# MLP first layers: the lo halves made by GpSimd from SBUF, their factor folded in at the start, and another share for the work beside attention

## Chip, core and metric

The kernel runs on one core of one Trainium2 chip. The metric is the time of the program on the device in microseconds (us). The engines are named as in the profile: PE is TensorE, DVE is VectorE, ACT is ScalarE, POOL is GpSimd, SP is SyncE, which issues the DMAs here.

## What is computed

The input x is 4 x 1024 x 256 in float32. Three residual steps follow each other: half a mixture-of-experts layer, a transformer block, and half the mixture-of-experts layer again.

```python
x = x + 0.5 * ffn(layernorm(x))
x = x + attn(layernorm(x))
x = x + 0.5 * ffn(layernorm(x))

# attn, per batch: 16 heads of 64, 1024 rows
q, k, v = (ln(x, s, b) @ W + bias for each of the three)
p = softmax(q @ k.T / 16 + mask)          # mask: one corner element, -999
h = (p @ v) @ Wo + bo + x
y = ln(h, lnm_s, lnm_b)
m = gelu(y @ W1 + b1) @ W2 + b2           # tanh form of gelu; W1 is 256 x 512
return m + h

# ffn: 8 experts with the best 2 weighted, and a shared one, 256 -> 128 -> 256, exact gelu
```

The change is in the line `m = gelu(y @ W1 + b1) @ W2 + b2`, the MLP of the transformer block.

## The kernel before

**Precision.** Matmul operands are split into two float16 numbers, hi and lo, where hi is the rounded value and lo the rest. A product is three matmuls: hi by hi, hi by lo, lo by hi (`mm3`, L974 to L978, whose matmuls all carry the line L970). Every operand made on the chip therefore costs two operations: one that writes hi and one that subtracts hi from the full value.

**Tiling.** A batch has 8 pairs of heads; for each pair q, k and v are projected, and then come 4 units (a head and a half of its queries) of 4 steps. In all there are 4 x 8 x 4 x 4 = 512 attention steps. A step i has these parts:

- `maxima` (L1444): scores of 128 queries into PSUM slot 0 (L1464), whose row maximum DVE takes (L1471). After four of them `row` (L1495) turns the maxima into a row (L1498, L1502) that a DMA puts into the tile `low`.
- `scores` (L1509): the transposed scores, already less the maximum, into PSUM slot 1 (L1528, L1529). ACT takes the exponential into `pt` (L1534, run in the helper at L570) and rounds it to `pk` hi (L1540). POOL makes `pk` lo, 128 x 1024 (L1543).
- `values` (L1564): 24 small matmuls of `pk` with V (L1578, L1580, L1581). The first two of each three need `pk` hi, the third needs `pk` lo. DVE normalises after four steps (L1593, L1594).

**Work beside attention.** Everything else is written as generators that ask for an engine and a duration (`yield Ask("DVE", 0.69)`) and are run by a planner, the class `Order` (L102). The planner fixes the order of the instructions on each engine when the program is built; it keeps a plan time per engine and takes the asks in the order of their readiness. Ahead of and behind the scores of each step, `order.share(SHARE)` (L1727, L1734) gives TensorE's plan a budget of SHARE us of other work: projections of the next pair, output projections (L1748), the expert layers of the next and the previous batch, and the MLP. Where attention isn't ready, other work is taken too. On POOL an ask of such a chain may go ahead of a waiting L1543 when that is made later by no more than LPOOL = 2.3 us of plan time (SLOW = 0.7 for rank 2).

**The resources.** PSUM has two slots of 1024 columns for scores, one place for values, and three banks of 512 columns, tag F, for all other work (`F_`, L332; `free`, L335, tells the planner that one is free). The SBUF tag `u` has BU = 3 buffers of 512 float32 columns, which MLP chunks and experts share.

**The MLP.** A job is half a batch, 512 rows. `prep` (L1837) makes the layernorm and the transposed input; it also loads x1d into `ld` buffers and lets POOL add it and the bias b2 to h (L1851, L1853). `burst` (L1856) runs the first layer in 4 chunks c of 128 hidden columns, each one bank of 512 rows, and starts a chain `gelu_tanh` (L1809) for each. `second` (L1880) runs the second layer in 4 tiles of 128 rows, each of which needs hi and lo of all 4 chunks. A chunk's chain before:

- L1814, ACT: the bank u becomes the layer's output, scaled, plus the bias `mb1`
- L1816, ACT: v (SBUF) = the square of u; L1818, DVE: v = (v + 1/c) u
- L1820, ACT: tanh of v (run at L570)
- L1822, DVE: u = (v + 1) u, in the bank
- L1824, ACT: hi = 8 u; L1826, DVE: lo = 8 u - hi; only then is the bank free (L1827)

There are 8 MLP jobs, 32 chunks. Those of the first three batches run beside attention; both of the last batch run behind the last value matmul, together with three halves of expert layers. The expert layers' own first layers (`layer`, L1128) already have their lo part made by POOL from SBUF (L1183) where they run beside attention.

**mb1.** `bias_cols` (L626) makes the bias of the first layer during the setup: a matmul, a DMA to memory and back, and a multiplication by a factor (L648), which is 1.0 here (L868).

Of the kernel before, what the change touches and what calls it, by code (L numbers as in the profile page):

```python
# [10 lines left out]
AF = mybir.ActivationFunctionType  # L11
ALU = mybir.AluOpType
# [12 lines left out]
MH = 512  # L25
EPS = 1e-5

CX = 4.0
# [6 lines left out]
CW1 = 32.0  # L35
CG = 16.0
# [14 lines left out]
KW = 8  # L51
RANK, RREST = -2, -3
WAIT, AGE, LATE, LPOOL, SLOW = 2.0, 0.2, 1.6, 2.3, 0.7
SHARE, RATE, LEAD, NEAR, OWED = 0.7, 0.58, 40, 20, -16.0
BLD = 2
BU = 3
BGB = 3
# [8 lines left out]
GELU_C = 0.044715  # L66
# [241 lines left out]
class Kernel:  # L308
# [342 lines left out]
    def setup(self):  # L651

        nc, a, cp, ap, order = self.nc, self.a, self.cp, self.ap, self.order
# [159 lines left out]
        def all_qkv():  # L813
            self.stored = [0] * 3
            order.start(qkv(0), -7)
            order.start(qkv(1), -7)
            order.start(qkv(2), -7)
            yield Ask("IF", lambda: sum(self.stored) == 6)
            order.start(others(), 5)
            yield Ask("IF", lambda: all(f"bias{n}" in self.biases for n in "qkv"))  # L820
            yield Ask("DMA", 3.0)
            self.bqkv = [self.biases[f"bias{n}"] for n in "qkv"]
            self.qkv_set = order.seen

        def kept(parts, dram, at):
            t = self.tile(ap, [P, 2, S], F16, "pk", bufs=BPK)

            def to():
                for l in range(2):
                    dma(dram[l, :, at:at + S], t[:, l])  # L830

            yield from self.split(parts, t[:, 0], t[:, 1], to)
            self.setup_left -= 1

        def others():

            self.wod = self.tile(self.dp, [2, P, 8 * D], F16, "wod")
            self.mwd = self.tile(self.dp, [2, P, 2 * 2 * MH], F16, "mwd")
            wo = [self.tile(ap, [P, S], F32, "pt", bufs=BPT)[:] for i in range(2)]
            for i in range(2):  # L840
                dma(wo[i].rearrange("p (c n) -> p c n", c=4), a["Wo"][i * 4 * P:(i + 1) * 4 * P, :].rearrange("(c p) n -> p c n", p=P))
            self.bo = self.row_bcast(a["bo"], D, "bo")
            s, bc = self.cols(a["lnm_s"], 2, "lnms"), self.cols(a["lnm_b"], 2, "lnmb")
            w1, w2 = self.tile(ap, [P, S], F32, "pt", bufs=BPT)[:], self.tile(ap, [P, S], F32, "at", bufs=BAT1)[:]
            dma(w1.rearrange("p (c n) -> p c n", c=2), a["W1"].rearrange("(c p) n -> p c n", p=P))
            dma(w2.rearrange("p (c n) -> p c n", c=4), a["W2"].rearrange("(c p) n -> p c n", p=P))
            self.mb2 = self.row_bcast(a["b2"], D, "mb2")
            yield Ask("DMA", 6.0)
            jobs = [([(wo[i], None, CWO)], self.wod, i * S) for i in range(2)]
            jobs.append(([(w1[:, k * MH:(k + 1) * MH], s[:, k:k + 1], CW1) for k in range(2)], self.mwd, 0))  # L850
            jobs.append(([(w2, None, CW2)], self.mwd, S))
            for job in jobs:
                order.start(kept(*job), 5)
            yield Ask("IF", lambda: self.qkv_set)
            bv = self.tile(ap, [P, NPAIR, P], F32, "aT", bufs=BAT)
            yield Ask("DVE", 1.1)
            nc.vector.tensor_copy(bv[:], self.bqkv[2][:].unsqueeze(2).to_broadcast([P, NPAIR, P]))
            yield Ask("BANK")
            ps = self.F_()[:, :D]
            for c in range(NPAIR):  # L860
                if c % 2 == 0:
                    yield Ask("PE", 0.9)
                nc.tensor.matmul(ps, bv[:, c, :], wo[c // 4][:, c % 4 * D:c % 4 * D + D], start=(c == 0), stop=(c == NPAIR - 1))
            yield Ask("DVE", 0.42)
            nc.vector.scalar_tensor_tensor(self.bo[:], ps, 1.0 / AV, self.bo[:], ALU.mult, ALU.add)
            self.free()
            self.bo_ready = order.seen
            order.start(self.bias_cols([w1[:, :MH], w1[:, MH:]], bc, 1.0, a["b1"], "mb1"), 5)  # L868
            yield Ask("IF", lambda: "mb1" in self.biases)
            self.mb1 = self.biases["mb1"]  # L870
            self.setup_left -= 1
# [937 lines left out]
    def gelu_tanh(self, u, c, hp, job):  # L1809

        nc = self.nc
        v = self.tile(self.mp, [P, 512], F32, "u", bufs=BU)[:]
        yield Ask("ACT", 0.67)
        nc.scalar.activation(u, u, AF.Identity, bias=self.mb1[:, c:c + 1], scale=1.0 / (CX * CW1))  # L1814
        yield Ask("ACT", 0.6)
        nc.scalar.activation(v, u, AF.Square)  # L1816
        yield Ask("DVE", 0.69)
        nc.vector.scalar_tensor_tensor(v, v, 1.0 / GELU_C, u, ALU.add, ALU.mult)  # L1818
        yield Ask("EXP", 0.63)
        self.tabled(v, v, AF.Tanh, scale=GELU_C * math.sqrt(2.0 / math.pi))  # L1820
        yield Ask("DVE", 0.69)
        nc.vector.scalar_tensor_tensor(u, v, 1.0, u, ALU.add, ALU.mult)  # L1822
        yield Ask("ACT", 0.6)
        nc.scalar.mul(hp[:, 0], u, CG / 2)  # L1824
        yield Ask("DVE", 0.69)
        nc.vector.scalar_tensor_tensor(hp[:, 1], u, CG / 2, hp[:, 0], ALU.mult, ALU.subtract)  # L1826
        self.free()  # L1827
        self.u_live -= 1
        job.left -= 1

# [97 lines left out]
```

## Time and profile before

| | us |
|---|---|
| median of 3 runs (2074.29 to 2075.26) | 2075.26 |
| profiled execution, its own time | 2072.14 |
| its span, first to last instruction | 2070.3 |
| TensorE busy in the span | 1968.2 |
| VectorE, ScalarE, GpSimd busy | 1411.7, 1500.8, 1498.1 |
| span up to the first `pk` lo (setup, first experts, first pair) | 161 |
| attention steps, to the last value matmul | 161 to 1918 |
| behind it: the last MLP and expert halves | 1918 to 2070.3 |
| mean granted TensorE clock, share of full | 0.989 |

The share of an engine is an average over stretches with different work. POOL, for example, is busy through the attention steps and almost idle behind 1918 us. Lines of groups read: line, engine, operation, output <- input, partitions x elements, count | busy us, mean ns of one | idle time of the engine just ahead of them, and what ended it. Lines of waits read: who waited, for whom: us in total, times, the longest.

### The profile page before, as it was taken

The page shows a single profiled execution, that of the slowest core. Times are in us where ns is not written, and L with a number is a line of the kernel's source. Part 1 is how long each engine was busy: PE and PEld are TensorE (multiplying, and loading weights), DVE is VectorE, ACT ScalarE, POOL GpSimd, SP SyncE. Part 2 cuts the span into 40 slices and gives each one's busy share as a digit, 9 for nine tenths or more (in the row PEclk, how much of TensorE's full clock was granted, in tenths as well). Part 3 has the DMA queues.
Part 4 walks back from the last instruction along what each step waited for, and adds up shares of the span by engine and source line. Part 5 has one row for each costly group of instructions (what it writes and reads, how often), then busy time and mean ns, then how long its engine had stood idle before and what let it go on. Part 6 is the DMA issues. An engine that isn't in the chain of part 4 may idle for free.

```text
span 2070.3 us, 53013 instructions
## 1 busy us (share of the span) xinstructions
PE 1968.2 (95%) x22468; PEld 1286.2 (62%) x22468; DVE 1411.7 (68%) x2372; ACT 1500.8 (72%) x1785; POOL 1498.1 (72%) x979
## 2 busy tenths in 40 slices
PE   6989999999999999999999999999999999999689
PEld 2546576766666566666666666656675666667356
DVE  6576676766767677776767568677677577764654
ACT  6437878778766787788787778687868787777553
POOL 7737787768767988778687987878776888778300
PEclk9999999999999999999999999999999999999899
DMA  6543233333613315243333333323233324241000
GB/s 174 151 128 84 75 91 95 76 85 68 143 35 80 86 32 113 48 113 73 85 81 81 95 75 80 96 70 75 70 69 92 103 46 107 50 103 27 21 1 31
DMA packets 213019, 166.21 MB, mean 80 GB/s; under 512 B 140991, under 2 KB 172872, under 8 KB 212782
## 3 DMA queue, kind: packets, MB, share of 16 engines
q1 hardware_dynamic: 212782, 162.83, 32.1%
q8 instruction: 176, 2.88, 0.6%
q14 instruction: 61, 0.50, 0.1%
HBM read 70.18 MB, written 13.83 MB: 41 GB/s over the span
## 4 chain that ended last, share of the span: by engine, by line
PE 79%; POOL 6%; ACT 5%; DVE 4%; DMA 3%; issue 2%; SPq 1%; POOLq 0%; DVEq 0%; ACTq 0%
PE F L970 31%; PE S L1528 10%; PE S L1464 10%; PE S L1529 9%; PE av L1581 6%; PE av L1580 5%; PE av L1578 5%; POOL pk L1543 3%; PE S L970 2%; ACT pt L570 1%; DMA gb<-gd 1%; ACT pk L1540 1%; POOL hp L1183 1%; PE S L1498 1%; POOL h L1851 1%
## 5 line engine op out<-in xcount | busy, mean ns | idle before, releaser
L1543 POOL TENSOR_TENSOR pk<-pt,pk 128x1024 f16<-128x1024 f32 x512 | 1087.8, 2133 | 258.7 <-ACT pk L1540 167.8
L1471 DVE TENSOR_REDUCE mx<-S 128x1 f32<-128x1024 f32 x512 | 626.1, 1223 | 305.4 <-PE S L1464 280.5
L570 ACT ACTIVATE pt<-S 128x1024 f32<-128x1024 f32 x512 | 523.8, 1023 | 355.4 <-PE S L1529 336.8
L1540 ACT CAST pk<-pt 128x1024 f16<-128x1024 f32 x512 | 534.7, 1045 | 15.8 <-DMA aT<-pk 0.6
L1581 PE MATMUL av<-V,pk 128*128 128x65 f16 x4096 | 428.8, 192 | 25.2 <-POOL pk L1543 24.1
L1580 PE MATMUL av<-V,pk 128*128 128x64 f16 x4096 | 435.1, 195 | 0.0
L1578 PE MATMUL av<-V,pk 128*128 128x65 f16 x4096 | 434.1, 193 | 0.7 <-DVE at L1594 0.7
L1578 PEld LDWEIGHTS <-pk 128*128 128x128 f16 x4096 | 382.1, 96 | 53.9 <-issue 0.3
L1580 PEld LDWEIGHTS <-pk 128*128 128x128 f16 x4096 | 380.4, 97 | 52.9 <-issue 1.1
L1581 PEld LDWEIGHTS <-pk 128*128 128x128 f16 x4096 | 379.9, 99 | 30.3 <-POOL pk L1543 30.0
L1528 PE MATMUL S<-low 128*128 128x512 f16 x1024 | 388.2, 379 | 6.2 <-ACT pt L570 5.5
L1529 PE MATMUL S<-AC 128*128 128x512 f16 x1024 | 388.4, 379 | 0.0
L1464 PE MATMUL S<-AC 128*128 128x512 f16 x1024 | 304.2, 378 | 8.2 <-DVE mrow L1502 4.8
L970 PEld LDWEIGHTS <-hp 128*128 128x128 f16 x2100 | 205.6, 98 | 78.2 <-issue 10.5
L970 PE MATMUL F<-xA,wq 128*128 128x512 f16 x768 | 187.6, 381 | 0.1
L970 PE MATMUL F<-wfs,hp 128*128 128x256 f16 x1404 | 178.0, 275 | 5.9 <-ACT u L570 3.7
L1529 PEld LDWEIGHTS <-AC 128*128 128x128 f16 x1024 | 99.9, 98 | 115.3 <-issue 27.6
L1528 PEld LDWEIGHTS <-low 128*128 128x128 f16 x1024 | 99.9, 98 | 104.0 <-issue 0.4
L1183 POOL TENSOR_TENSOR hp<-u,hp 128x512 f16<-128x512 f32 x88 | 100.7, 1159 | 78.5 <-ACT hp L1180 71.9
L970 PEld LDWEIGHTS <-wfs 128*128 128x128 f16 x864 | 84.3, 99 | 109.7 <-issue 20.7
L970 PE MATMUL F<-xF,wfs 128*128 128x512 f16 x522 | 127.1, 388 | 5.7 <-DVE gb L642 4.2
L970 PEld LDWEIGHTS <-wq 128*128 128x128 f16 x768 | 74.9, 98 | 84.6 <-issue 2.6
(239 smaller groups left out, 2544.8 us busy)
## 6 DMA issues: line engine op xcount, KB each, us to landing
AC<-qk SPq DMA_DIRECT2D x128, 256.0 KB
gb<-gd SPq DMA_DIRECT2D x88, 256.0 KB
low<-qk SPq DMA_DIRECT2D x64, 256.0 KB
wq<-wqd SPq DMA_DIRECT2D x33, 384.0 KB
hp<-mwd SPq DMA_DIRECT2D x6, 1024.0 KB
x<-in_L_attn_x_dram SPq DMA_DIRECT2D x8, 512.0 KB
x1d<-x SPq DMA_DIRECT2D x8, 512.0 KB
wo<-wod SPq DMA_DIRECT2D x16, 256.0 KB
```

The lines of the kernel that those rows point to most:

```text
L570: i = self.nc.scalar.activation(out, in_, func, **kw).ins
L970: i = self.nc.tensor.matmul(*args, start=start, **kw).ins
L1183: nc.gpsimd.tensor_tensor(hp[e][:, 1], u, hp[e][:, 0], ALU.subtract)
L1464: mm(ps[:, hs], AC[:, 0, qs], AC[:, 1, hs], start=True, stop=(h == 0 or t > 0), skip_group_check=True)
L1471: nc.vector.tensor_reduce(self.mx[:, t % 4:t % 4 + 1], ps, AX.X, ALU.max, negate=True)
L1528: mm(o, low[:, 1, ks], low[:, 0, qs], start=True, stop=False, skip_group_check=True)
L1529: mm(o, AC[:, 1, ks], AC[:, 0, qs], start=False, stop=True, skip_group_check=True)
L1540: nc.scalar.copy(pk[:, 0], pt[:])
L1543: nc.gpsimd.tensor_tensor(pk[:, 1], pt[:], pk[:, 0], ALU.subtract)
L1578: mm(o[:, 0:65], pk[:, 0, ps], v[:, 0:65], start=(n == 0 and c == 0 and t == 0), stop=False, skip_group_check=True)
L1580: mm(o[:, 0:64], pk[:, 0, ps], v[:, 65:129], start=False, stop=False, skip_group_check=True)
L1581: mm(o[:, 0:65], pk[:, 1, ps], v[:, 0:65], start=False, stop=(n == 3 and c == 1), skip_group_check=True)
```

## The change

The chunk's chain carries the factor 8 from its beginning, DVE's second operation writes v in SBUF and not the bank, the bank is freed there, hi is a plain copy of v, and POOL subtracts hi from v to make lo. `mb1` gets the same factor. SHARE goes from 0.70 to 0.68.

```diff
-SHARE, RATE, LEAD, NEAR, OWED = 0.7, 0.58, 40, 20, -16.0
+SHARE, RATE, LEAD, NEAR, OWED = 0.68, 0.58, 40, 20, -16.0
...
-            order.start(self.bias_cols([w1[:, :MH], w1[:, MH:]], bc, 1.0, a["b1"], "mb1"), 5)
+            order.start(self.bias_cols([w1[:, :MH], w1[:, MH:]], bc, CG / 2, a["b1"], "mb1"), 5)
...
         yield Ask("ACT", 0.67)
-        nc.scalar.activation(u, u, AF.Identity, bias=self.mb1[:, c:c + 1], scale=1.0 / (CX * CW1))
+        nc.scalar.activation(u, u, AF.Identity, bias=self.mb1[:, c:c + 1], scale=CG / 2 / (CX * CW1))
         yield Ask("ACT", 0.6)
-        nc.scalar.activation(v, u, AF.Square)
+        nc.scalar.activation(v, u, AF.Square, scale=2 / CG)
...
-        self.tabled(v, v, AF.Tanh, scale=GELU_C * math.sqrt(2.0 / math.pi))
+        self.tabled(v, v, AF.Tanh, scale=2 / CG * GELU_C * math.sqrt(2.0 / math.pi))
         yield Ask("DVE", 0.69)
-        nc.vector.scalar_tensor_tensor(u, v, 1.0, u, ALU.add, ALU.mult)
+        nc.vector.scalar_tensor_tensor(v, v, 1.0, u, ALU.add, ALU.mult)
+        self.free()
         yield Ask("ACT", 0.6)
-        nc.scalar.mul(hp[:, 0], u, CG / 2)
-        yield Ask("DVE", 0.69)
-        nc.vector.scalar_tensor_tensor(hp[:, 1], u, CG / 2, hp[:, 0], ALU.mult, ALU.subtract)
-        self.free()
+        nc.scalar.copy(hp[:, 0], v)
+        yield Ask("POOL", 1.16)
+        nc.gpsimd.tensor_tensor(hp[:, 1], v, hp[:, 0], ALU.subtract)
         self.u_live -= 1
         job.left -= 1
```

CG is 16. The lines after the change: the copy is L1825 and POOL's subtraction L1827. The buffer v is in use until that subtraction has read it; the counter `u_live` counts it to the end of the chain, before and after.

## The prediction

> **What bounds the kernel now.** I read the page first: busy shares, slices, the chain that ended last.
>
> ```profile
> span 2070.3 us, 53013 instructions
> PE 1968.2 (95%) x22468; PEld 1286.2 (62%) x22468; DVE 1411.7 (68%) x2372; ACT 1500.8 (72%) x1785; POOL 1498.1 (72%) x979
> PE   6989999999999999999999999999999999999689
> POOL 7737787768767988778687987878776888778300
> PE 79%; POOL 6%; ACT 5%; DVE 4%; DMA 3%; issue 2%; SPq 1%; POOLq 0%; DVEq 0%; ACTq 0%
> ```
>
> TensorE is busy 95% of the span and makes 79% of the chain; it is full but for the first and the last slices. The change leaves its 22468 matmuls as they are, so only its idle time, 2070.3 - 1968.2 = 102 us, can move. The table by stretches places it: 30.1 us between 715 and 1918 us (1203.0 less 1172.9 busy), and 28.3 us behind 1918 us, after the last value matmul (152.3 less 124.0). Before 715 us nothing changes (see below). Next, the waits of TensorE:
>
> ```profile
> PE av L1581 <- POOL pk L1543: 24.1, 24, 1.7
> PE S L1528 <- ACT pt L570: 5.5, 13, 1.1
> PE S L1464 <- DVE mrow L1502: 4.8, 7, 0.9
> PE F L970 <- DVE hp L1826: 2.0, 2, 1.8
> PE F L970 <- DVE pt L1826: 0.7, 1, 0.7
> ```
>
> The columns are us in total, times, longest. The largest named wait is that of the value matmuls (L1581) for the lo parts that POOL makes (L1543): 24 times. So POOL, 72% busy, is the engine whose lateness TensorE feels most, and the change gives it more work. The waits that the change can take away, for a PSUM bank held until L1826, are two, 1.75 and 0.70 us of the last two lines (the third, 0.2 us, is for the lo part itself), both behind 1918 us.
>
> The groups give the prices (busy and mean ns, then idle before and its releaser):
>
> ```profile
> L1543 POOL TENSOR_TENSOR pk<-pt,pk 128x1024 f16<-128x1024 f32 x512 | 1087.8, 2133 | 258.7 <-ACT pk L1540 167.8 <-issue 29.5 <-PE S L1529 22.9
> L1183 POOL TENSOR_TENSOR hp<-u,hp 128x512 f16<-128x512 f32 x88 | 100.7, 1159 | 78.5 <-ACT hp L1180 71.9 <-PE S L1529 4.8
> L1180 ACT CAST hp<-u 128x512 f16<-128x512 f32 x88 | 52.4, 613 | 14.1 <-DVE u L1168 14.1
> L1822 DVE SCALAR_TENSOR_TENSOR F<-u,F 128x512 f32<-128x512 f32 x32 | 22.0, 688 | 8.8 <-ACT u L570 8.3
> L1826 DVE SCALAR_TENSOR_TENSOR hp<-F,hp 128x512 f16<-128x512 f32 x28 | 19.0, 683 | 3.8 <-ACT hp L1824 3.6
> L1824 ACT ACTIVATE hp<-F 128x512 f16<-128x512 f32 x28 | 16.4, 591 | 0.3 <-DVE F L1822 0.3
> ```
>
> Last, the six stretches in which MLP first layers run beside attention; the columns are stretch, its length, then busy us (and instructions) of PE, PEld, DVE, ACT and POOL, the granted clock, DMA share, GB/s:
>
> ```profile
> 731.10:762.20 31.10, 29.04 (x337) 17.24 (x336) 23.64 (x33) 26.24 (x35) 26.10 (x19) 1.00 0.18 43
> 1351.30:1401.20 49.90, 46.98 (x584) 29.96 (x583) 37.43 (x52) 45.93 (x60) 38.31 (x19) 1.00 0.30 73
> 1646.70:1685.00 38.30, 36.77 (x440) 22.35 (x439) 28.89 (x41) 32.46 (x40) 36.17 (x28) 1.00 0.23 53
> sum 243.40, PE 232.89 PEld 145.63 DVE 183.34 ACT 211.13 POOL 191.56; mean PE 38.81 PEld 24.27 DVE 30.56 ACT 35.19 POOL 31.93
> ```
>
> Here TensorE is idle 10.5 us of 243, and 8.3 of these are waits for L1543. ACT is the fullest helper (211 of 243), POOL next (192).
>
> **The change part by part.** There are 32 chunks of 512 columns (8 MLP halves of 4): 24 in the six stretches, 8 behind 1918 us.
>
> (1) DVE loses the 32 lo operations (28 in the row above, 4 more into other tiles): 32 x 0.683 = 21.9 us, 24 x 0.683 = 16.4 in the six stretches. DVE is not the bound there (183 of 243). Idle of TensorE there that is not L1543's is 10.5 - 8.3 = 2.2 us; the gain lies between 0 and 2.2. I take 0.7, since only the waits for a row maximum are DVE's.
>
> (2) The hi part becomes a copy from SBUF instead of a scaled read of PSUM: 613 ns (L1180) for 591, 24 x 0.022 = 0.5 us on ACT, which stands ahead of L1540. Between 0 and 0.5; 0.3 taken. L1822 writes SBUF: its neighbour L1818, which does so, takes 0.680 for 0.688. The new scale operands (L1816, the tanh) and mb1's factor stand in instructions that ran before: 0, as no instruction is added; mb1's own is one of 0.135 us at 154.8 us.
>
> (3) The bank is free after L1822, not after L1826. In the 24 chunks that is 4.2 us earlier of 13.1 us (means from the start of L1814). TensorE waited for no such bank before 1918 us, so the gain there is 0; if one becomes the limit, it is at most those 2.2 us.
>
> (4) POOL gains 32 x 1.159 = 37.1 us (L1183 is the same operation), 24 x 1.159 = 27.8 in the six stretches: 191.6 + 27.8 = 219.4 of 243.4, still below the stretch. But two stretches run over: 26.1 + 4.6 = 30.7 of 31.1, and 36.2 + 4.6 = 40.8 of 38.3, where the 16 operations L1304 and L1309 of the next batch's h fall too. The queue behind an added operation is L1543, and behind that the value matmuls; the buffer v is also held until POOL is done. To price it, I took the order in which the instructions of both programs stand. For each attention step I summed the TensorE work between the end of its scores and its first value matmul (its cover, at 0.217 us per 512 columns, as in runs of 12 matmuls in 2.59 us), and the other POOL work queued just ahead of its L1543. Then I read from the trace what each kind of step waits for L1543, over steps 8 to 511:
> cover under 5.3 us with other POOL work ahead: 18 steps, 13.88 us, 0.771 each; after: 23 steps.
> cover under 5.3 us, none ahead: 57 steps, 0.056 each; after: 54.
> longer cover, over 1.7 us ahead: 41 steps, 0.133 each; after: 42.
> the rest: 388 steps, 0.009 each; after: 385.
> So 25.9 us become 17.7 + 3.0 + 5.6 + 3.3 = 29.6, +3.7. With the cover cut finer (at 4.3, 5.3 and 6.1 us) it is 27.3, +1.5. I take +2.0, nearer the finer cut. Bounds: -4 (half of the 8.3 gone, as the order is another one) and +11 (24 x 0.46, the rate of the finer class with a cover of 4.3 to 5.3 us and over 1.7 us of other POOL work ahead).
>
> The Trainium skill speaks against this part: "GPSIMD Engine Reference", Engine selection, puts elementwise work of two inputs on VectorE, GpSimd being about 2x slower. The rows here say 1159 for 683 ns, 1.7x. By the rule, each move costs the difference, and 24 of them in line would be 11 us slower; by the rows above, POOL has room in four of six stretches and the sum is +2.
>
> (5) The share 0.68. The order of the changed program is that of before until the 169th score step, near 740 us, on TensorE and likewise on the others: no effect before it. Behind it, with the lo parts moved and the share left at 0.70, the same count gives 35 to 38 us of waits; with the share at 0.68 alone, 25 to 27. So the share takes back most of what POOL's load costs, and (4) holds it already. The work left behind the last value matmul is 818 matmuls in both, so nothing is pushed to the end: 0.
>
> (6) Behind 1918 us POOL does next to nothing, but its queue matters. Gains: the bank waits of 1.75 us (the matmuls at 1938.10) and 0.70 us go; six matmuls of the fourth chunk move up into the wait of 4.37 us at 1929.8. Cost: POOL's order puts the second chunk's lo behind both L1851, which start at 1938.37 once their loads have landed, and the third's behind both L1853: 1938.37 + 2.68 + 1.16 = 1942.2, then + 2.48 + 1.16 = 1945.8. The second layer's first tile needs the third's lo at its ninth matmul, and the transposes behind it, at 1943.47 before, start near 1946.1: 2.6 us late, and with them the router's chain. Its end was a wait of 3.37 us of TensorE (L1162 on L1073); now 12 matmuls of 512 columns, 2.6 us, stand ahead of it. The two cancel: 0, bounds -3 (the bank waits gone, the delay covered) and +5 (not covered, and the fourth lo late too).
>
> The sum against the profiled run's 2072.14 us (2070.3 of span and 1.8 around it): 2072.14 + 2.0 + 0.3 - 0.7 + 0 = 2073.7, +1.6 us. The median of the three runs is 2075.26, so the changed one's would be 2076.9; I write 2077. 0.2% of it is 4.15 us, about what a measurement of this kernel can tell from no change: 2071.1 to 2079.4.
>
> **Rivals.**
> Slower: POOL becomes what the value matmuls wait for. Its place: the two overfull stretches, and the score step after the ffn block around 1150 us, where 17.65 us of other POOL work now stand ahead of one L1543 (16.20 before) with a cover of 4.7 us (7.9 before), next one 3.5. Price: a full operation for one chunk in three, 8 x 1.16 = 9.3, less 0.7: 2084. It decides once POOL's idle time before L1543 in these stretches is gone. For it: 24 waits on POOL already. Against: four stretches with room.
> Faster: banks and DVE freed early let other work fill the gaps. Half of the 10.5 us idle in the six stretches and the 2.45 us of bank waits: -7.7, 2067.6. For it: banks are held 13.1 us and three must serve everything. Against: no wait for a bank is seen before 1918 us.
> The change does nothing but reorder: waits of 24 in all are scattered, and another order can shift the same sum either way by some us; it lies in the forecast's own range.
> The share costs: work starved in attention and left for the end, one pair's 8 us of projections: 2083. Against: the same 818 matmuls at the end.
>
> **How the numbers follow.** Forecast (about even, own range 2072 to 2081) 0.43: of it 0.36 within 0.2%, 0.07 slower. POOL bound 0.25, slower. Share 0.03, slower. Freed banks 0.29, faster. So faster 0.29, same 0.36, slower 0.35. The bounds of the parts sum to -9 and +16; the range keeps 2067 to 2087, leaving out some 0.1 on each side.
>
> **What would show it.** In the changed profile: L1826 gone from DVE, 32 operations of about 1.16 us on POOL, POOL near 1535 us busy, DVE near 1390; TensorE's waits for L1543 at 25 to 28 us; the value waits between 715 and 1918 us, not the tail, carrying the difference; the second and third lo near 1942 and 1946 if the tail starts where it did. I am wrong if the waits for L1543 fall by several us, if they pass 33, or if the stretch behind the last value matmul changes by more than 4 us.

## The result, and the profile after

The changed kernel takes 2076.9 us (median of 21 runs, 2075.69 to 2080.14), the kernel before, in 21 runs beside them, 2072.65. The ratio is 1.0021, 95% interval 1.0015 to 1.0027: 0.2% slower, 4.25 us. The forecast of 2077 stood on the earlier median of 2075.26 and on +1.6; the time came out as written because the base was 2.6 too high and the step 2.65 too small, which is luck. The two profiled executions differ by 2076.24 - 2072.14 = 4.1 us. First the page of the changed kernel, its busy shares, slices of TensorE and POOL, and chain:

```profile
span 2074.5 us, 52994 instructions
PE 1966.3 (95%) x22468; PEld 1286.1 (62%) x22468; DVE 1392.9 (67%) x2340; ACT 1501.5 (72%) x1785; POOL 1533.4 (74%) x1011
PE   6989999999999999999999999999999999999788
POOL 7737787768767998787777888877776898777500
PE 80%; POOL 6%; ACT 5%; DVE 3%; DMA 3%; issue 3%; SPq 1%; POOLq 0%; DVEq 0%; ACTq 0%
```

The work moved as forecast: DVE does 32 instructions and 18.8 us less, POOL 32 and 35.3 us more, TensorE's matmuls are the same 22468. The groups (busy us, mean ns, then idle before) give the prices that were used:

```profile
L1827 POOL TENSOR_TENSOR hp<-u,hp 128x512 f16<-128x512 f32 x28 | 32.4, 1160 | 15.3 <-ACT hp L1825 15.2
L1822 DVE SCALAR_TENSOR_TENSOR u<-u,F 128x512 f32<-128x512 f32 x32 | 21.7, 679 | 9.4 <-ACT u L570 9.4
L1825 ACT CAST hp<-u 128x512 f16<-128x512 f32 x28 | 17.2, 614 | 0.3 <-DVE u L1822 0.3
```

1160 ns for the lo part and 614 for the copy were forecast as 1159 and 613. So no price of an operation was off, and the step of the time lies in waits and, at the end, in the clock. TensorE's waits in the changed kernel (us in total, times, longest):

```profile
PE av L1581 <- POOL pk L1543: 28.6, 26, 3.5
...
PE S L1464 <- DVE mrow L1502: 10.7, 13, 0.9
PE S L1528 <- ACT pt L570: 5.6, 12, 1.1
PE F L970 <- DVE u L1822: 4.8, 5, 1.6
```

The waits for POOL's lo rose from 24.1 to 28.6. The line that matters more stood in the prediction's own fence and was passed over: a score matmul that waits for the row of maxima, from 4.8 us in 7 waits to 10.7 us in 13. Last, the stretches, cut at each kernel's own last value matmul: before, which ends attention at 1917.8 us,

```profile
715.00:1917.80 1202.80, 1172.90 (x14314) 779.09 (x14312) 839.43 (x1306) 930.49 (x1058) 954.23 (x568) 1.00 0.33 78
1917.80:2070.30 152.50, 123.99 (x819) 78.28 (x818) 86.56 (x208) 76.70 (x131) 17.36 (x27) 0.90 0.06 18
```

and after, which ends it at 1926.6:

```profile
715.00:1926.60 1211.60, 1174.52 (x14316) 779.88 (x14314) 826.34 (x1283) 931.42 (x1058) 980.82 (x592) 1.00 0.32 77
1926.60:2074.50 147.90, 121.61 (x818) 78.32 (x818) 81.48 (x200) 76.84 (x131) 26.41 (x35) 0.92 0.06 19
```

The first number behind the stretch is its length. Attention is 8.8 us longer with the same matmuls, the end 4.6 us shorter: +4.2 in all (the spans differ by 2074.5 - 2070.3). Two opposite moves, each larger than the sum, stand behind the 0.2%.

**Where attention lost.** From 161 us to the last value matmul TensorE is idle 42.5 us before and 50.0 after, +7.5. Of this the waits for L1543 give +4.5 and those for the row +5.9; those of L1464 and L1498 for the maxima (L1471) fall from 3.9 to 1.5, -2.4; smaller ones make up the rest. The remaining 1.3 us are longer busy times of matmuls, whose ends are modelled. One of the 13 waits for the row, in the timeline of the changed kernel (start, us, engine, line; some rows between are left out):

```profile
835.74 0.19 PE L1581 MATMUL av<-V,pk 128*128 128x65 f16 x1
835.77 0.27 PE L1498 MATMUL S<-ident,mx 128*4 128x128 f32 x1
835.97 0.18 DVE L1593 RECIPROCAL rc<-av 128x4 f32<-128x4 f32 x1 [1.68 <-PE av L1581]
836.26 0.42 DVE L1594 TENSOR_TENSOR at<-av,rc 128x256 f32<-128x256 f32 x1
836.60 0.27 DVE L1502 TENSOR_SCALAR mrow<-S 4x128 f16<-4x128 f32 x1
836.92 0.59 PE L1464 MATMUL S<-AC 128*128 128x512 f16 x2 [0.88 <-DVE mrow L1502]
```

The transpose of the maxima (L1498) writes PSUM slot 0, the slot into which the next maxima (L1464) go. Here nothing stands between the two on TensorE. DVE first normalises the values (L1593, L1594), then reads the row (L1502), and TensorE stands for 0.88 us. Such a transpose is called bare below. It can be counted in the order of the instructions, without a run: 7 bare transposes before, 13 after. What one costs depends on DVE's order. Where DVE has other work ahead of the row, as here the normalising, TensorE waits 0.81 to 0.90 us (12 of the 13 after). Where DVE reads the row as soon as the transpose ends, it waits 0.37 us (one after, two of the 7 before):

```profile
1825.24 0.27 PE L1498 MATMUL S<-ident,mx 128*4 128x128 f32 x1
...
1825.55 0.28 DVE L1502 TENSOR_SCALAR mrow<-S 4x128 f16<-4x128 f32 x1
...
1825.88 0.59 PE L1464 MATMUL S<-AC 128*128 128x512 f16 x2 [0.37 <-DVE mrow L1502]
```

These lines are from the kernel before.

The single longest wait for POOL looks like the prediction's slower rival in one place. POOL's timeline after, ahead of a value matmul that waits 3.47 us at 1391.59:

```profile
1385.09 1.16 POOL L1827 TENSOR_TENSOR hp<-u,hp 128x512 f16<-128x512 f32 x1
1386.21 1.16 POOL L926 TENSOR_TENSOR xs<-ld,xs 128x512 f16<-128x512 f32 x1
1387.32 2.13 POOL L1411 TENSOR_TENSOR pk<-at,pk 128x1024 f16<-128x1024 f32 x1
1389.40 6.30 POOL L1543 TENSOR_TENSOR pk<-pt,pk 128x1024 f16<-128x1024 f32 x3
```

The added operation and two others, 4.4 us, stand ahead of L1543. From 1390.84 us, inside this wait, TensorE's granted clock is 0.5 for 3.4 us, the only such interval in attention after 715 us; before has none. TensorE is busy 2.66 us in it; with the double time at half clock that the end shows below, about 1.3 of these are extra (an estimate), about what the matmuls' busy time grew by.

**Where the end gained.** TensorE's timeline before, behind the last value matmul:

```profile
1934.18 2.17 PE L939 MATMUL S<-ident,ld 128*128 128x128 f32 x8 [4.37 <-ACT ld L919]
1938.10 2.74 PE L970 MATMUL F<-xF,qk 128*128 128x512 f16 x6 [1.75 <-DVE hp L1826]
...
1963.35 1.01 PE L1162 MATMUL S<-gt,sel 128*128 128x512 f16 x2 [3.37 <-DVE gt L1073]
```

and after, where the same work begins 8.8 us later:

```profile
1940.39 1.47 PE L970 MATMUL F<-xF,qk 128*128 128x512 f16 x6 [1.48 <-DVE u L1822]
1943.13 1.91 PE L939 MATMUL S<-ident,ld 128*128 128x128 f32 x8 [1.27 <-ACT ld L919]
...
1947.35 0.40 PE L970 MATMUL F<-qk,hp 128*128 128x256 f16 x1 [0.84 <-POOL hp L1827]
...
1970.38 0.59 PE L1162 MATMUL S<-gt,sel 128*128 128x512 f16 x2 [0.56 <-DVE gt L1073]
```

The six matmuls of the fourth chunk have moved up into the wait of 4.37 us, of which 1.48 and 1.27 are left, and the router's wait of 3.37 is 0.56. The waits for a PSUM bank didn't go: before, two of them last 2.45 us behind the last value matmul (for L1826), after, five last 4.8 us (for L1822). They stand in other places, while the two longest waits became 5.9 us shorter together. The same six take 1.47 us for 2.74: before, they ran at half clock. Worked out from windows of 1 us (twice what their granted clock lacks to 1), the end has half clock for 30.7 us before and 24.9 after. So of the 4.6 us, 2.2 are idle time (28.5 to 26.3) and 2.4 are shorter matmuls (123.99 to 121.61).

The Trainium skill, "TensorE: Matmul & The Clock Gate", section "What's actually happening", puts the half clock down to at least one idle window of about 3.4 us. The wait of 4.37 us agrees with that. In the wait of 3.47 us the half clock begins after 2.7 us already, and where it begins after at 1947.2 us, no wait in the 12 us ahead of it is longer than 1.48 us, though there were several. So here it also followed shorter waits.

### The profile page after: what moved, and what is told of

Read it like the earlier page. It is cut to its first block, busy times and chain, and to the rows that moved or that the text cites. A ratio compares the mean times of both kernels' runs of the same rounds, so it can differ in the third digit from the quotient of the medians.

```text
span 2074.5 us, 52994 instructions
## 1 busy us (share of the span) xinstructions
PE 1966.3 (95%) x22468; PEld 1286.1 (62%) x22468; DVE 1392.9 (67%) x2340; ACT 1501.5 (72%) x1785; POOL 1533.4 (74%) x1011
## 4 chain that ended last, share of the span: by engine, by line
PE 80%; POOL 6%; ACT 5%; DVE 3%; DMA 3%; issue 3%; SPq 1%; POOLq 0%; DVEq 0%; ACTq 0%
PE F L970 31%; PE S L1528 10%; PE S L1464 10%; PE S L1529 10%; PE av L1581 6%; PE av L1580 5%; PE av L1578 5%; POOL pk L1543 3%; PE S L970 2%; ACT pt L570 1%; DMA gb<-gd 1%; ACT pk L1540 1%; POOL hp L1183 1%; PE S L1498 1%; POOL h L1851 1%
## 5 line engine op out<-in xcount | busy, mean ns | idle before, releaser
L1543 POOL TENSOR_TENSOR pk<-pt,pk 128x1024 f16<-128x1024 f32 x512 | 1087.2, 2133 | 233.6 <-ACT pk L1540 141.1
L1471 DVE TENSOR_REDUCE mx<-S 128x1 f32<-128x1024 f32 x512 | 626.2, 1223 | 316.1 <-PE S L1464 287.4
L1581 PE MATMUL av<-V,pk 128*128 128x65 f16 x4096 | 429.3, 193 | 29.6 <-POOL pk L1543 28.6
L1581 PEld LDWEIGHTS <-pk 128*128 128x128 f16 x4096 | 380.3, 99 | 34.8 <-POOL pk L1543 34.5
L1528 PE MATMUL S<-low 128*128 128x512 f16 x1024 | 388.4, 379 | 6.2 <-ACT pt L570 5.6
L1464 PE MATMUL S<-AC 128*128 128x512 f16 x1024 | 304.9, 379 | 12.7 <-DVE mrow L1502 10.7
L1528 PEld LDWEIGHTS <-low 128*128 128x128 f16 x1024 | 100.1, 98 | 104.4 <-issue 1.1
L1183 POOL TENSOR_TENSOR hp<-u,hp 128x512 f16<-128x512 f32 x88 | 100.7, 1158 | 77.9 <-ACT hp L1180 71.1
```

Source lines behind the costliest of these rows:

```text
L1183: nc.gpsimd.tensor_tensor(hp[e][:, 1], u, hp[e][:, 0], ALU.subtract)
L1464: mm(ps[:, hs], AC[:, 0, qs], AC[:, 1, hs], start=True, stop=(h == 0 or t > 0), skip_group_check=True)
L1471: nc.vector.tensor_reduce(self.mx[:, t % 4:t % 4 + 1], ps, AX.X, ALU.max, negate=True)
L1528: mm(o, low[:, 1, ks], low[:, 0, qs], start=True, stop=False, skip_group_check=True)
L1543: nc.gpsimd.tensor_tensor(pk[:, 1], pt[:], pk[:, 0], ALU.subtract)
L1581: mm(o[:, 0:65], pk[:, 1, ps], v[:, 0:65], start=False, stop=(n == 3 and c == 1), skip_group_check=True)
```

## The experiments

All ratios are to the kernel before, run on the same chip beside them. "Order" is the order in which the planner lays the instructions on each engine; it is read from the program, without a run.

**The change's two halves apart.** The diff is against the changed kernel. tail_only gives the new chain to the last 8 chunks alone; the other 24 keep DVE's lo from the bank (with the factor folded in and hi a plain copy), and the share stays 0.70. The order ahead of the last value matmul is that of before. att_only is its mirror (`if not last`), with the share 0.68.

```diff
-    def gelu_tanh(self, u, c, hp, job):
+    def gelu_tanh(self, u, c, hp, job, last):
...
+        if last:
...
+            nc.vector.scalar_tensor_tensor(v, v, 1.0, u, ALU.add, ALU.mult)
+            self.free()
...
+            nc.scalar.copy(hp[:, 0], v)
...
+            nc.gpsimd.tensor_tensor(hp[:, 1], v, hp[:, 0], ALU.subtract)
+        else:
...
+            nc.vector.scalar_tensor_tensor(u, v, 1.0, u, ALU.add, ALU.mult)
...
+            nc.scalar.copy(hp[:, 0], u)
...
+            nc.vector.tensor_tensor(hp[:, 1], u, hp[:, 0], ALU.subtract)
+            self.free()
```

> Share 0.70 and the chunk's chain as before in the 24 chunks beside attention (hi a copy, the factor folded in, lo by VectorE from the bank), the new chain only in the 8 chunks behind the last value matmul; the order up to there is that of before. Theory (the new chain is worth 4 to 5 us behind the last value matmul, and costs 8 us ahead of it): the stretch behind it falls from 152.5 to 148 us, ratio to before 0.9977 to 0.9983. Rival (the shorter end stretch of the changed kernel is only work that its later last value matmul had let run ahead): the stretch stays at 151 to 153 us, ratio 0.999 to 1.001.

> The changed kernel, share 0.68, with the chunk's chain of before in the 8 chunks behind the last value matmul. Order ahead of it as in the changed kernel. Theory: last value matmul at 1925 to 1928 us, the stretch behind it 152 us, ratio to before 1.0035 to 1.0045. Rival (the end stretch is short in any case after a late last value matmul): ratio 1.0015 to 1.0025.

tail_only: 2068.77 us, 0.998 (0.9972 to 0.9989). Its last value matmul ends at 1917.7 us (1917.8 before), the stretch behind it lasts 146.0 us (152.5). It is faster than both kernels. att_only: 2079.98 us, 1.0045 (1.0032 to 1.0057); the last value matmul ends at 1926.4, the stretch behind it lasts 151.5. So the loss belongs to attention and the gain to the end, and the two add up within their intervals: -0.0020 and +0.0045 against +0.0021 for both.

**The lo parts and the share apart.** lo70 is the changed kernel with the share back at 0.70; share68 is the kernel before with 0.68.

```diff
-SHARE, RATE, LEAD, NEAR, OWED = 0.68, 0.58, 40, 20, -16.0
+SHARE, RATE, LEAD, NEAR, OWED = 0.7, 0.58, 40, 20, -16.0
```

> The changed kernel with the share of before, 0.70. By the count of steps with a short cover and other POOL work ahead (32, against 23 and 18) it waits 35 to 38 us for L1543 instead of 27 to 30: ratio to the changed kernel +0.3 to +0.5%, to before 1.005 to 1.007. Rival (the share does nothing to the waits; POOL's load makes them): as the changed kernel, 1.0015 to 1.0027. Rival (the share of 0.68 is what costs): 0.999 to 1.001.

> Before with a share of 0.68 and nothing else. By the count of steps its waits for L1543 are 25 to 27 us, as before: ratio 0.999 to 1.001. Rival (the share costs): 1.002 or more. If the lo parts alone cost the time, this is not slower than before.

lo70: 2087.11 us, 1.0077 (1.0064 to 1.0089), last value matmul at 1940.7. share68: 2086.18 us, 1.0075 (1.0062 to 1.0089), at 1931.0. TensorE's waits in share68:

```profile
PE av L1581 <- POOL pk L1543: 28.7, 23, 3.9
...
PE S L1464 <- DVE mrow L1502: 10.4, 14, 0.9
```

These are nearly the two lines of the changed kernel, and here no lo part has moved: POOL's work is that of before. The share alone makes attention 13.2 us longer, the lo parts alone 22.9, both together 8.8. The parts don't add, so neither has a price of its own: with either, the planner lays all that follows anew.

**Load or order.** light keeps the order of the changed kernel up to the last value matmul, but beside attention POOL subtracts 32 of the 512 columns; the rest of those lo parts is left out and stays zero (one clearing by DVE for each job). heavy (the second part of the diff) does each of the 24 subtractions twice; the planner doesn't know of the second.

```diff
-        nc.gpsimd.tensor_tensor(hp[:, 1], v, hp[:, 0], ALU.subtract)
+        n = 512 if job.last else 32
+        nc.gpsimd.tensor_tensor(hp[:, 1, :n], v[:, :n], hp[:, 0, :n], ALU.subtract)
...
         nc.gpsimd.tensor_tensor(hp[:, 1], v, hp[:, 0], ALU.subtract)
+        if not job.last:
+            nc.gpsimd.tensor_tensor(hp[:, 1], v, hp[:, 0], ALU.subtract)
```

> The changed kernel, planned order ahead of the last value matmul the same, but GpSimd makes only 32 of the 512 columns of each lo part beside attention (the rest is zero, by one VectorE memset per job; the lo parts of the MLP's first layers are left out there). Takes some 24 x 0.9 us off GpSimd and keeps its place and its waits. Theory (the order that the planner now makes costs the time, not GpSimd's load): last value matmul at 1924 to 1928 us, ratio to before 1.0012 to 1.0025. Rival (GpSimd's load in that order costs it): last value matmul at 1916 to 1921 us, ratio 0.996 to 0.999.

> The changed kernel with each of the 24 lo subtractions beside attention done twice: the same order on TensorE, ScalarE and VectorE, 24 x 1.16 = 27.8 us more on GpSimd. Theory (order, not load): under 3 us on the last value matmul, 1926 to 1930 us. Rival (load): as much again as the change cost, 8 us or more, 1934 us or later, and waits for L1543 over 34 us.

light: 2077.31 us, 1.0022 (1.0012 to 1.0032), last value matmul at 1926.4 for 1926.6. Its waits (two lines are added above, so L1583 and L1466 are L1581 and L1464):

```profile
PE av L1583 <- POOL pk L1545: 26.1, 24, 2.6
...
PE S L1466 <- DVE mrow L1504: 10.7, 13, 0.9
```

POOL has 24 x (1158 - 246) ns = 21.9 us less to do, by the two rows of that line, and TensorE waits 2.5 us less for L1543, but neither the time nor the end of attention is better beyond what two executions can differ by. The 13 bare transposes are all there. Taking the load away didn't bring the end of attention back to 1918 us or near it: it is the order that costs most of the 8.8 us. How much is the load's can be told only to some 3 us, by which executions of one order differ (see tail_dve below). The total says less, as light's order behind the last value matmul is another one and lasts 151.3 us there, 3.4 longer than after's. (The clearing by DVE is 6 x 0.91 us; the profiled execution lies 2.2 us above light's median.) The wait of 3.47 us lasts 2.6 in light (the longest of the first line), so 0.9 us of it was the load; share68, where no lo part has moved, has one of 3.9. heavy: 2090.84 us, 1.0089 (1.0076 to 1.0103), last value matmul at 1943.1, waits for L1543 of 41.5 us in 39. Here the theory of the order alone failed: a second 27.8 us of POOL costs 16.5 us. This order has room on POOL for one operation per chunk where it was planned, not for a second that the plan doesn't know.

**What shortens the end.** tail_dve is tail_only with the last 8 chunks' lo made by DVE, from SBUF; the ask to the planner stays that for POOL.

```diff
-            nc.gpsimd.tensor_tensor(hp[:, 1], v, hp[:, 0], ALU.subtract)
+            nc.vector.tensor_tensor(hp[:, 1], v, hp[:, 0], ALU.subtract)
```

> As tail_only (new chain in the last 8 chunks alone, share 0.70), but there VectorE makes lo, from v in SBUF: the bank is freed early, GpSimd has nothing of it. Theory (the early bank is what shortens the end): 145 to 148.5 us behind the last value matmul, ratio to before 0.997 to 0.999, as tail_only. Rival (the work taken off VectorE is what shortens it): 150 to 153 us, ratio 0.9995 to 1.0005.

2068.52 us, 0.9982 (0.9973 to 0.9991), the stretch behind the last value matmul 146.1 us (tail_only 146.0). Up to there its order is that of before, as tail_only's is, yet it ends attention at 1920.7 us, 2.9 later: so much can one profiled execution differ from another in attention without any change, and smaller differences there aren't read. The engine of the lo part doesn't matter there; what both have is the bank freed behind the second DVE operation. The folded factor and the plain copy of hi aren't the cause: att_only's last chunks have them too, in the order of before, and its end lasts 151.5 us. But the early bank alone isn't enough. In every kernel of the table below with a short end (145.9 to 147.9 us) the fourth chunk's six matmuls stand ahead of the transposes, in the wait of 4.37 us. In light, whose last chunks have the new chain as well, they stand behind the first four of the eight:

```profile
1943.11 0.44 PE L941 MATMUL S<-ident,ld 128*128 128x128 f32 x2 [3.97 <-ACT ld L921]
1944.12 0.44 PE L941 MATMUL S<-ident,ld 128*128 128x128 f32 x2 [0.57 <-ACT ld L921]
1944.40 2.71 PE L972 MATMUL F<-xF,qk 128*128 128x512 f16 x6
```

The long wait is back, the six matmuls run at half clock, and the end lasts 151.3 us. The early bank makes the better order possible; it doesn't ensure it. The clock is part of it: the end has half clock for 17.8 us in tail_only and 21.0 in tail_dve, 30.7 before. This sum isn't a measure of the time by itself, as att_only, in the order of before, has 35.8 us of it and an end 1 us shorter. The windows of before in which the waits of 4.37 and 3.37 us end show it (granted clock third from the end),

```profile
1933.80:1941.80 8.00, 5.87 (x22) 2.81 (x22) 3.62 (x6) 6.44 (x14) 4.69 (x6) 0.57 0.24 66
1960.80:1968.80 8.00, 5.46 (x15) 2.02 (x15) 4.65 (x7) 6.68 (x12) 0.00 (x0) 0.57 0.00 0
```

and tail_only where the second one would be:

```profile
1950.00:1965.00 15.00, 10.77 (x55) 4.81 (x53) 10.81 (x36) 13.76 (x24) 5.38 (x8) 1.00 0.00 0
```

**Can the order be read beforehand?** Three more shares, after the two counts (bare transposes, and steps with a short cover and other POOL work ahead of L1543) had been fitted to the runs above: tail_64 and tail_80 are tail_only with the share 0.64 and 0.80, after_64 is the changed kernel with 0.64.

```diff
-SHARE, RATE, LEAD, NEAR, OWED = 0.7, 0.58, 40, 20, -16.0
+SHARE, RATE, LEAD, NEAR, OWED = 0.64, 0.58, 40, 20, -16.0
```

> As tail_only, share 0.64. In its order 11 row transposes (7 in before, 13 in the changed kernel) have no TensorE work between them and the next maxima, and 18 steps (18, 23) have a short cover with other GpSimd work ahead. Theory (an order's price can be read from these two counts: 0.88 us for each bare transpose, 0.77 us for each such step): last value matmul 3 us later than before, 1921, and the end stretch of tail_only: ratio to before 0.9995 to 1.0005. Rival (any other order than the tuned one costs about 10 us, whatever the counts): last value matmul at 1926 or later, ratio 1.002 or more.

> As tail_only, share 0.80: 20 bare transposes and 30 steps with a short cover and other GpSimd work ahead. Theory (the counts): 11.4 + 9.7 = 21 us later than before at the last value matmul, 1939, ratio to before 1.0065 to 1.0095. Rival (any other order costs about 10 us): 1925 to 1932, ratio 1.001 to 1.004.

> The changed kernel with a share of 0.64: 12 bare transposes and 23 steps with a short cover, nearly the counts of the changed kernel (13 and 23). Theory (the counts): last value matmul at 1924 to 1929 us, ratio to before 1.0015 to 1.0035. Rival (the orders scatter whatever the counts): off by more than 5 us either way, ratio under 1.000 or over 1.005.

| kernel | ratio | last value matmul, us | behind it, us | waits for L1543, us | waits for the row, us (times) | bare, counted |
|---|---|---|---|---|---|---|
| before | 1 | 1917.8 | 152.5 | 24.1 | 4.8 (7) | 7 |
| tail_only | 0.998 | 1917.7 | 146.0 | 25.4 | 4.8 (7) | 7 |
| after_64 | 0.9999 | 1924.5 | 146.9 | 25.7 | 9.2 (12) | 12 |
| after | 1.0021 | 1926.6 | 147.9 | 28.6 | 10.7 (13) | 13 |
| tail_64 | 1.0019 | 1929.0 | 146.0 | 24.4 | 8.1 (11) | 11 |
| share68 | 1.0075 | 1931.0 | 152.6 | 28.7 | 10.4 (14) | 13 |
| lo70 | 1.0077 | 1940.7 | 145.9 | 30.0 | 11.0 (15) | 15 |
| tail_80 | 1.0159 | 1954.8 | 147.5 | 35.2 | 15.8 (20) | 20 |

The count of bare transposes gives the waits for the row in all eight kernels, to one. The whole isn't read from it. after_64 ended attention where it was forecast, but its ratio (0.9990 to 1.0008) lies below the forecast, at the edge of what the rival named. tail_64 ends attention 11.2 us behind the kernel before where 3 were forecast, with a ratio of 1.0009 to 1.0028, nearer to its rival, and tail_80 37 where 21 were, with 1.0142 to 1.0176, past theory and rival. So 8 and 16 us lie in neither count. Part shows as waits of L1528 for the exponential (4.8 us before, 7.1 in share68, to the last value matmul), part as half clock at long waits (after 715 us none before, 3.4 us after, 10.3 in tail_80), part as longer busy times of matmuls, in which the half clock counts again (TensorE busy from 161 us to the last value matmul: 1714.3 before, 1717.9 in share68, 1723.5 in lo70). What sets this rest stays open. All six re-planned orders of the table end attention 6.7 to 37 us later than the order of before.

## Right and wrong, step by step

(1) and (2), DVE -0.7 and ACT +0.3: the durations came as forecast. TensorE's waits for the maxima fell by 2.4 us, a little past the bound of 2.2; whether that is DVE's relief or the other order wasn't separated. ACT's effect can't be seen: waits of L1528 for the exponential are 4.8 before and 5.0 after.

(3), the bank freed early brings 0 before 1918 us: no run contradicts it, and none has the early bank beside attention in the order of before, so it wasn't measured by itself.

(4), POOL's load at +2.0: the waits for L1543 rose by 4.5, above the coarser count (+3.7; its classes began at 25.9 us where the profile names 24.1), and 28.6 lies just past the 25 to 28 named, below the 33 that would have refuted it. The term was mis-sized, and so was its cause: light takes most of the load away and attention ends where it did. More of the loss lay in a wait that had no term in the sum. The re-planned order has six more bare transposes, 5.9 us. The line `PE S L1464 <- DVE mrow L1502: 4.8, 7, 0.9` was shown, and the changed order could be read before the run; only steps ahead of L1543 were counted in it. With the sum's own terms plus six at that line's mean of 0.69 us the forecast for attention would have been 1.6 + 4.1 = 5.7, and at 0.88, the price that most of them have in the changed kernel, 6.9, against 8.8 measured.

(5), "the share takes back most of what POOL's load costs": half right. From lo70 to the changed kernel it does bring 14.1 us of attention. But the waits for L1543 are 30.0 and 28.6 there, where 35 to 38 and 27 to 30 had been counted, so it isn't POOL's load that is taken back. And the share at 0.68 alone, forecast at no change, costs 13.2 us. The rival "the share costs" had named another mechanism, work left for the end, which didn't come: the same 818 matmuls stand behind the last value matmul in share68.

(6), the end at 0 with bounds -3 and +5: wrong, -4.6, past the bound and past the 4 us named as the refutation. Of the gains, the fourth chunk did move into the wait of 4.37 us; the bank waits didn't go but grew from 2.45 us to 4.8. The cost that was to cancel the gains didn't reach TensorE. The second and third lo started half a microsecond later than the sum has it (1941.05 and 1944.7): at 1950.42 and 1953.98 us, which less 8.8 is 1941.6 and 1945.2. But the transposes that were to start 2.6 us late begin at 1950.48, less 8.8 is 1941.7, against 1943.47: 1.8 us early, as ten of the second layer's matmuls stand ahead of them for 18 before, and these didn't need the third lo. The only wait of a matmul for L1827 is 0.84 us. And the sum had no term for the clock, half of the gain in these two executions.

So the range and the middle case held by luck, through errors that cancel: attention 7 us too cheap, the end 4.6 too dear, and a base 2.6 too high. The slower rival (POOL the bound) isn't what happened, though heavy shows how near it lies. The faster rival had the freed banks fill the gaps beside attention; they did so only behind it. The rival "nothing but reorder" is the nearest to what the runs show, but it was given no price of its own and taken to move the sum by some us either way; the six new orders here are all later, by 6.7 to 37 us. By the Trainium skill's rule weighed in step (4) ("GPSIMD Engine Reference", Engine selection) the moves would have cost 11 us in line. In light, with most of that work left out, attention ends 0.2 us earlier, so where they were planned the operations cost no more than the 3 us that can't be told apart here.

## What to carry to other kernels

Where a planner lays out the whole program, one changed ask can change every later place, so the order is the change: compare the two orders for every round trip between engines that loses its cover, each at the price its wait has in the trace, and not only for the queue that gets the new work. Here even that named only part of the loss. Test a move in two steps, the new order without the load and the load without the new order, before a price is put on the load. And take the part that is local: freeing the bank early in the last eight chunks leaves the order ahead of it alone and is the version that beats both kernels (2068.77 us, 0.998).

## What was not expected of the hardware

A transpose whose result VectorE must read before the next scores may be written costs TensorE 0.37 us when nothing stands between and VectorE is free, and 0.81 to 0.90 us when VectorE normalises or does other work first, though the two operations last 0.27 us each. TensorE's clock counted as much as its waits at the end: matmuls of 512 columns went from six in 2.74 us to six in 1.47, with 30.7 us at half clock before and 17.8 in tail_only. GpSimd's subtraction isn't all per-column: 1158 ns for 512 columns, 246 for 32, so, from these two sizes, 1.9 ns a column and some 185 ns that stay.
